# Routing eight late token tiles at the end of an attention, with a new weight layout, send order and pace of adds in the expert layer behind it

## The chip, the cores and the metric

The kernel runs on one core of a Trainium2 chip. The metric is the device time of one execution in microseconds (us). The core has engines that run their own instruction lists side by side: PE (TensorE, the matrix multiplier; PEld is its loading of weights), DVE (VectorE), ACT (ScalarE), POOL (GpSimd) and SP (SyncE, which here only issues transfers). An engine runs its list strictly in order: an instruction that waits for another engine or for a transfer (DMA) holds all that stand behind it. Transfers are carried by 16 DMA engines that all queues share.

## The reference, cut to what matters

The program is a stack of residual layers over 4096 tokens of 256 numbers, all in float32. The last one, which this change is about, is a mixture of 16 experts, of which each token uses four:

```python
x = x + _L1_attn_ref(_layernorm(x), ...)             # 16 heads, 8 sequences of 512 tokens
x = x + 0.5 * _L1_ffn_ref(_layernorm(x), ...)

def _L1_ffn_ref(x, gate_w, w1, w2, w3, ws1, ws2, ws3):
    scores = softmax(x @ gate_w.T)                   # 16 experts in 4 groups
    # keep the 2 groups with the largest best score, then the 4 best experts in them
    c = the scores of those four, 0 elsewhere        # [tokens, 16]
    a = silu(einsum('td,edi->tei', x, w1)) * einsum('td,edi->tei', x, w3)     # 128 hidden per expert
    y = einsum('tei,eid,te->td', a, w2, c)
    z = silu(x @ ws1) * (x @ ws3) @ ws2              # the shared expert, 256 hidden
    return y + z
```

Ahead of it stand an expert layer of another kind, an attention, the first expert layer again, this mixture of experts for a first time, and the attention named above (called the second attention here).

## The kernel before, in words

Tokens are held in SBUF as `x`, 32 *token tiles* of 128 tokens, one token on each of 128 partitions; four token tiles are a *group* (0 to 7, group 7 the last). A layer norm takes mean and variance of each row (`ln_mean`), then the inverse root of the variance, either with ACT's square root (`ln_root`, `ln_rest`) or with a shift and three Newton steps on DVE (`ln_guess`), and then normalizes the rows (`normal`).

*The second attention* (2236 to 3462 us in the profile) goes through 8 sequences. Between its matmuls it works off a list `todo` of small pieces, one or two per half chunk: adds of the previous mixture (`one.add`), means, roots, normalizations. It also routes the last layer ahead: the last layer's token tiles are cut into *part 0*, the first 20, and *part 1*, the last 12 (`LAST = 20, 12`). Once five sequences are through, `after.routing(0, ...)` runs piece by piece, and part 0's rows are sent. Logits of part 1's first eight tiles are also ready before the attention ends (`after.lg1`); those of the last four need the last sequence, whose output projection `project` is the attention's last work.

*Routing* (`Joint.routing`) is a generator that runs on DVE nearly alone; each `yield` is a place where the caller may put other work. It takes the softmax, picks two groups and four experts by repeated maximum (`topk`), counts each expert's tokens with two matmuls against constant triangles, works out for each token and each of its four experts a *slot*, and then `owner` (which expert a slot tile belongs to) and `coef` (the scores, halved). A slot tile is 128 slots of one expert. 143 slot tiles are held; part 0 fills tiles 0 to 63 for sure, tiles 64 to 95 take rows of both parts, tiles from 96 on have rows of part 1 alone.

*Sends* (`Joint.send`) write the normalized rows to their slots in DRAM: four indirect transfers from POOL per token tile, 48 for part 1. Each waits for the one before the last to have landed.

*The last layer* (`ffn1_after`, 3462 to 3889 us) has an order written out by hand, in which each engine's list is the order of the calls. In this order:

- SP's list: the weights of four experts, the first four loads of slot tiles (`xs`), the other experts' weights, the shared expert's weights.
- The tile loop, `for i in range(total)`: pass i is `step(i)`, which handles a pair of slot tiles at each of four stages: `hide(i-2)` multiplies with w1 and w3 and applies silu, `back(i-3)` transposes, `turn(i)` transposes the loaded rows, `give(i-4)` multiplies with w2 and writes the result `ys` to DRAM. So there are 72 pairs and 76 passes. Three results per pass are copied out of PSUM by `evict`, which alternates between DVE and ACT. Pair 32 is the first that is loaded after the sends of part 1 (its loads are issued in `turn(32)` and wait for all 48), and pass 51 is the one that writes pair 47, the last one with rows of part 0 (`known` is 48).
- Between the first passes: the root and normalization of group 7 after pass 2, its transposes (`columns`) and logits, and `routing(1, ...)`, four yields a pass; when it ends, the 48 sends are issued. The other groups are normalized again from then on, one every second pass.
- *Gathers and adds*: for each token tile four indirect transfers from POOL bring the four experts' rows into a buffer `yg` (four buffers), and four DVE instructions (line 1614) add them to `x` with their coefficients. `fetched(at)` does half of this: an even call adds the first half of the token tile three places earlier, an odd call adds the second half and issues the gather of a token tile. In the tile loop this starts at pass `known + 3`, in two of three passes, for part 0's 20 tiles at most.
- After the passes the shared expert, as 32 *units* that a `Pump` runs one by one (a unit's PE work goes ahead of the previous unit's DVE work): 8 groups of two `hidden` and two `outputs` units. Between units the remaining `fetched` calls are spread evenly. When a token tile has got both its adds and its shared part, it is written out (`done`).

## Time and profile before

| | us |
|---|---|
| four timed runs | 3902.15, 3902.30, 3903.89, 3892.21 |
| their median | 3902.23 |
| profiled execution | 3890.69 |
| its span, first to last instruction | 3889.0 |

The span by stages (columns: us, then busy time and instructions of PE, PEld, DVE, ACT and POOL, the granted clock of PE as a share of full speed, mean busy share of the 16 DMA engines, GB/s):

```profile
0.00:1750.00 1750.00, 1614.89 (x8912) 977.11 (x8912) 674.28 (x2291) 587.58 (x944) 594.18 (x498) 0.96 0.30 78
1750.00:2236.00 486.00, 407.32 (x1894) 322.39 (x1895) 228.76 (x549) 116.83 (x244) 216.04 (x221) 0.88 0.51 161
2236.00:3462.00 1226.00, 1215.34 (x5793) 655.50 (x5793) 749.04 (x1178) 644.58 (x1518) 238.26 (x215) 1.00 0.06 18
3462.00:3889.00 427.00, 371.54 (x1697) 290.53 (x1693) 210.26 (x482) 101.22 (x216) 198.69 (x208) 0.93 0.55 168
```

The rows are: the layers ahead, the mixture of experts for the first time, the second attention, and the last layer. PE is busy for 99% of the attention; in the last layer it stands for 55 of 427 us, its clock is a little below full there, and the DMA engines are busy for more than half of the time.

Two groups of instructions that the change touches (line, engine, operation, output and inputs, count, busy time, mean ns of one, idle time of the engine just before them and what ended it):

```profile
L1857 POOL DMA_INDIRECT slots_d<-wide,slot  x48 | 47.1, 980 | 131.3 <-DVE slot L1979 96.9 <-DMA slots_d<-wide,slot 27.8 <-issue 6.7
L2010 POOL DMA_INDIRECT yg<-ys_d,slot  x128 | 134.4, 1050 | 118.3 <-DMA ys_d<-ys 75.4 <-issue 32.6 <-DVE x L1614 3.8
```

The first are part 1's sends: POOL waited 96.9 us for slots and 27.8 us for earlier sends to land. The second are the gathers: POOL waited 75.4 us for the tile loop's results, and nearly no time for the adds.

### The profile page before, as it was taken

The page shows a single profiled execution, that of the slowest core. Times are in us where ns is not written, and L with a number is a line of the kernel's source. Part 1 is how long each engine was busy: PE and PEld are TensorE (multiplying, and loading weights), DVE is VectorE, ACT ScalarE, POOL GpSimd, SP SyncE. Part 2 cuts the span into 40 slices and gives each one's busy share as a digit, 9 for nine tenths or more (in the row PEclk, how much of TensorE's full clock was granted, in tenths as well). Part 3 has the DMA queues.
Part 4 walks back from the last instruction along what each step waited for, and adds up shares of the span by engine and source line. Part 5 has one row for each costly group of instructions (what it writes and reads, how often), then busy time and mean ns, then how long its engine had stood idle before and what let it go on. Part 6 is the DMA issues. An engine that isn't in the chain of part 4 may idle for free.

```text
span 3889.0 us, 51805 instructions
## 1 busy us (share of the span) xinstructions
PE 3609.1 (93%) x18293; PEld 2245.5 (58%) x18293; DVE 1862.3 (48%) x4500; ACT 1450.2 (37%) x2922; POOL 1247.2 (32%) x1142
## 2 busy tenths in 40 slices
PE   4999998999995999999769999999999999988988
PEld 1666664555542666666458845555555555557865
DVE  7221206666555221217324556666555567546355
ACT  3222223444444222222113355555554555532321
POOL 2333324333421333325832212220000102723177
PEclk7999999999997999998879999999999999999999
DMA  5444532001012233324446500000000000135564
GB/s 191 116 129 133 142 79 69 21 23 28 18 40 88 66 76 72 73 46 132 138 136 218 178 22 28 28 28 6 1 1 1 1 1 16 72 114 173 169 182 128
DMA packets 258173, 309.32 MB, mean 80 GB/s; under 512 B 34048, under 2 KB 227968, under 8 KB 257664
## 3 DMA queue, kind: packets, MB, share of 16 engines
q1 hardware_dynamic: 182144, 177.78, 14.6%
q0 software_dynamic: 49152, 101.24, 10.7%
q10 hardware_dynamic: 26624, 27.00, 2.1%
q8 instruction: 151, 2.47, 0.3%
q14 instruction: 102, 0.84, 0.1%
HBM read 159.51 MB, written 138.02 MB: 77 GB/s over the span
## 4 chain that ended last, share of the span: by engine, by line
PE 45%; issue 4%; DVE 3%; DMA 2%; POOL 2%; another core or an unknown queue 1%; ACT 1%; SPq 0%; POOLq 0%; DVEq 0%; ACTq 0%
PE sp L1110 6%; PE tp L1130 6%; PE pq L1088 6%; PE zp L1157 6%; PE hs L1786 3%; PE pv L1077 3%; PE hs L2073 3%; PE yp L1172 3%; PE yps L1808 2%; PE yps L2095 1%; PE hp L1708 1%; POOL yg L2010 1%; PE tpx L1772 1%; PE rp L1144 1%
## 5 line engine op out<-in xcount | busy, mean ns | idle before, releaser
L521 PE MATMUL hp<-exT,w 128*128 128x512 f32 x1024 | 451.8, 595 | 0.7 <-issue 0.7
L552 PE MATMUL op<-w,hid 128*128 128x256 f32 x2048 | 451.9, 379 | 0.0
L1119 ACT ACTIVATE ex<-sp,nmax 128x512 f32<-128x512 f32 x512 | 344.7, 685 | 238.9 <-DVE nmax L1116 230.5
L552 PEld LDWEIGHTS op<-w,hid 128*128 128x128 f32 x2048 | 386.8, 190 | 64.1 <-issue 14.3
L557 DVE TENSOR_TENSOR ob<-op,b 128x256 f32<-128x256 f32 x128 | 54.4, 425 | 642.8 <-PE op L552 535.0
L1116 DVE TENSOR_REDUCE nmax<-sp 128x2 f32<-128x1024 f32 x256 | 301.6, 1220 | 81.4 <-PE sp L1110 79.3
L531 POOL DMA_INDIRECT acc_d<-ob,idx x128 | 201.7, 1576 | 419.3 <-ACT ob L558 353.3
L812 DVE CUSTOM_DVE_ANT_0 junk<-sp,mask 128x128 bf16<-128x128 f32 (+3 forms) x512 | 251.1, 491 | 166.1 <-PE sp L803 142.0
L521 PEld LDWEIGHTS hp<-exT,w 128*128 128x128 f32 x1024 | 192.2, 190 | 220.4 <-issue 216.8
L1130 PEld LDWEIGHTS tp<-ident,ex 128*128 128x128 f32 x2048 | 233.9, 141 | 145.4 <-issue 87.3
L525 ACT ACTIVATE hid<-hp,b 128x512 f32<-128x512 f32 x256 | 175.9, 687 | 315.5 <-PE hp L521 315.5
L1130 PE MATMUL tp<-ident,ex 128*128 128x128 f32 x2048 | 272.9, 275 | 6.6 <-ACT ex L1119 4.1
L1601 POOL DMA_INDIRECT yg<-ys_d,slot x128 | 129.6, 1013 | 427.3 <-DVE x L1614 271.6
L1110 PE MATMUL sp<-qk,qk 64*128 64x512 f32 x1024 | 254.4, 615 | 0.0
L1088 PE MATMUL pq<-xnT,wide 128*128 128x512 f32 x512 | 247.5, 607 | 1.2 <-ACT xnT L250 0.8
L252 DVE COPY eT<-tp 128x512 f32<-128x512 f32 x256 | 177.0, 691 | 140.5 <-PE tp L1130 139.4
L1157 PE MATMUL zp<-eT,v 128*64 128x512 f32 x1024 | 234.0, 598 | 0.0
L250 ACT COPY eT<-tp 128x512 f32<-128x512 f32 x256 | 149.7, 585 | 220.5 <-PE tp L1130 189.6
L492 POOL DMA_INDIRECT ex<-xn_d,idx x128 | 131.4, 1026 | 294.7 <-DVE idx L483 260.6
L558 ACT ACTIVATE ob<-ob,gate 128x256 f32<-128x256 f32 x128 | 65.0, 508 | 414.0 <-DVE ob L557 364.0
L1059 POOL TENSOR_TENSOR x<-x,xn 128x1024 f32<-128x1024 f32 x8 | 18.9, 2362 | 544.7 <-DVE xn L1054 544.7
L855 ACT ACTIVATE ex<-st 128x1024 f32<-128x1024 f32 x160 | 155.1, 1022 | 95.0 <-PE st L848 95.0
(432 smaller groups left out, 6057.4 us busy)
## 6 DMA issues: line engine op xcount, KB each, us to landing
xs<-slots_d SPq DMA_DIRECT2D x149, 256.0 KB
ys_d<-ys SPq DMA_DIRECT2D x149, 256.0 KB
w<-in_W SPq DMA_DIRECT2D x32, 1024.0 KB
slots_d<-zero ACTq DMA_DIRECT2D x7, 2304.0 KB
w_sb<-in_w SPq DMA_DIRECT2D x24, 512.0 KB
xn_d<-xn SPq DMA_DIRECT2D x16, 512.0 KB
acc_d<-x SPq DMA_DIRECT2D x16, 512.0 KB
x<-acc_d SPq DMA_DIRECT2D x16, 512.0 KB
```

What stands on the lines that cost most here:

```text
L252: self.nc.vector.tensor_copy(out, in_)
L521: nc.tensor.matmul(hp, lhsT=w1[:, c, f * P : f * P + P], rhs=exT[e][:, c, h * CH : h * CH + CH], start=(c == 0), stop=(c == DC - 1),)
L525: nc.scalar.activation(hid[h][:, f, :], hp, AF.Gelu, bias=b1[:, e, f : f + 1])
L531: inst = nc.gpsimd.indirect_dma_start(out=acc_d[:, :], out_offset=bass.IndirectOffsetOnAxis(ap=idx[:, e, st : st + 1], axis=0), in_=ob, in ...
L552: nc.tensor.matmul(op, lhsT=hid[h][:, f, i * P : i * P + P], rhs=w2[:, f, :], start=(f == 0), stop=(f == FC - 1),)
L812: nc.vector.tensor_tensor_reduce(out=junk[:, :wd], in0=sps[h // 2][:, h % 2, at : at + wd], in1=mask[:, S - wd :], scale=1.0, scalar=NEG, ...
L1088: nc.tensor.matmul(pp, lhsT=(wq, wk)[a][:, k, c * P : c * P + P], rhs=xnT[b][:, k, :], start=(k == 0), stop=(k == DC - 1),)
L1110: nc.tensor.matmul(sp[:, j, :], lhsT=q[r, qt * P : qt * P + P], rhs=k[r, :], start=True, stop=True)
L1116: nc.vector.tensor_reduce(nmax, sp, AX.X, ALU.max, negate=True)
L1119: nc.scalar.activation(ex[:, j, :], sp[:, j, :], AF.Exp, bias=nmax[:, j : j + 1], accum_out=ch["sums"][:, qt, j : j + 1],)
L1130: nc.tensor.transpose(tp[:, k, :], ch["ex", qt][:, j, k * P : k * P + P], self.ident)
L1157: nc.tensor.matmul(zp[DK1 * j : DK1 * j + DK1, :], lhsT=v[b, h][:, k, at : at + DK1], rhs=ch["eT"][:, j, k, :], start=(k == 0), stop=(k == ...
```

## The change

1. The attention's roots use `ln_guess` in three pieces instead of ACT's square root in two; `ln_guess` becomes a generator `ln_guesses` for that.
2. The expert weights lie in DRAM by partition: w1 and w3 side by side in one array `w13`, w2 transposed. A load of four experts is two transfers instead of three. In the last layer SP issues w13 of twelve experts, the four loads of slot tiles, w13 of the last four, w2 in two halves, and then the shared expert's weights.
3. The choice of experts (`choose`, the first part of what was `routing`) runs for part 1's first eight tiles at the end of the attention, in turn with the last four `project` calls, eight yields each. `kept` gives its results a place that lasts (one of the `yg` buffers), and `Cut` makes buffers of full size of which a part is used. `routing(1, ...)` chooses for the last four tiles alone and then goes on for all twelve.
4. In the last layer pass 2 is issued after the root and normalization of group 7. While routing runs, `lean` sends all three evictions of a pass to ACT. Routing takes six yields a pass up to pass 6, then three, instead of four.
5. Sends of part 1: each waits for the third one before it instead of the second, and POOL clears a small buffer (`pause`) after every four. The last group's token tiles are sent first, and groups 5 and 6 are normalized within the list of sends.
6. Adds begin at pass `known + 5`. Between the shared expert's units at most one `fetched` call follows a unit, three in four units; what is left comes after the last unit.

The diff, cut to this:

```diff
@@ Kernel
     def ln_guess(self, pool, stats, t0, n):
+        for _ in self.ln_guesses(pool, stats, t0, n):
+            pass
+
+    def ln_guesses(self, pool, stats, t0, n):
...
             nc.vector.scalar_tensor_tensor(new, u, 1.5, y, ALU.add, ALU.mult)
             y = new
+            yield
@@ attn1
         def roots(ranges):
-            ys = []
-
-            def first():
-                for stats, t0, n in ranges:
-                    ys.append(self.ln_root(pool, stats, t0, n))
-
-            def second():
-                for (stats, t0, n), y in zip(ranges, ys):
-                    self.ln_rest(pool, stats, t0, n, y)
-            return [first, second]
+            guesses = [self.ln_guesses(pool, stats, t0, n) for stats, t0, n in ranges]
+            return [lambda g=g: next(g, None) for g in guesses for _ in range(3)]
...
+        after.kept()
+        ready = after.parts[1] - QT
+        early = after.choose(
+            after.lg1[:, :ready], Cut(front.pool, after.parts[0]), after.score1[:, :ready], after.hots1[:, :, :ready]
+        )
         for i in range(QT):
+            advance(early, 8)
             project(B - 1, i)
             self.ln_mean(self.late, after.stats, (B - 1) * QT + i)
+        for _ in early:
+            pass
@@ Grouped
-    def expert_weights(self, groups=range(4)):
+    def expert_weights(self, groups=range(4), back=True):
...
-            nc.sync.dma_start(
-                out=self.w13[:, es, :, 0:INTER], in_=w["w1"][es].rearrange("e (c p) i -> p e c i", p=P)
-            )
-            nc.sync.dma_start(
-                out=self.w13[:, es, :, INTER:], in_=w["w3"][es].rearrange("e (c p) i -> p e c i", p=P)
-            )
-            nc.sync.dma_start(out=self.w2[:, es], in_=w["w2"][es].rearrange("e p d -> p e d"))
+            nc.sync.dma_start(out=self.w13[:, es], in_=w["w13"][:, es])
+            if back:
+                nc.sync.dma_start(out=self.w2[:, es], in_=w["w2"][:, es])
+
+    def back_weights(self):
+        nc, w = self.k.nc, self.k.w
+        for h in range(2):
+            es = slice(h * 8, h * 8 + 8)
+            nc.sync.dma_start(out=self.w2[:, es], in_=w["w2"][:, es])
@@ Joint
     def send(self, h, t, row):
...
-            before = self.sent[-2:-1]
+            before = self.sent[-2:-1] if h == 0 else self.sent[-3:-2]
...
+        if h == 1:
+            nc.gpsimd.memset(self.pause, 0.0)
+
+    def kept(self):
+
+        t = self.k.late.tile([P, TOPK, D], F32, name="yg", bufs=2).rearrange("p r d -> p (r d)")
+        n = self.parts[1] * E1
+        self.score1 = t[:, :n].rearrange("p (t e) -> p t e", e=E1)
+        self.hots1 = t[:, n : n + TOPK * n].rearrange("p (r t e) -> p r t e", r=TOPK, e=E1)
...
+    def routing(self, h, lg, pool, row_psum, chosen=0):
...
+        if h == 0:
+            score = pool.tile([P, HT, E1], F32, name="score")
+            hots = pool.tile([P, TOPK, HT, E1], F32, name="hots")
+        else:
+            score, hots = self.score1, self.hots1
+        yield from self.choose(
+            lg[:, chosen:], Cut(pool, HT), score[:, chosen:], hots[:, :, chosen:]
+        )
@@ tile_steps: turn, back, give
-            k.evict(st[j]["xT"][:, :n], tp[:, :n], j)
+            k.evict(st[j]["xT"][:, :n], tp[:, :n], j | self.lean)
...
-            k.evict(st[j]["aT"][:, :n], tp[:, :n, :P], j)
+            k.evict(st[j]["aT"][:, :n], tp[:, :n, :P], j | self.lean)
...
-            k.evict(ys[:, :n], yp[:, :n], j + 1)
+            k.evict(ys[:, :n], yp[:, :n], (j + 1) | self.lean)
...
+class Cut:
+    def __init__(self, pool, room):
+        self.pool, self.room = pool, room
+
+    def tile(self, shape, dtype, name, bufs=1):
+        axis = 2 if len(shape) == 4 else 1
+        n, full = shape[axis], list(shape)
+        full[axis] = self.room
+        t = self.pool.tile(full, dtype, name=name, bufs=bufs)
+        return t[:, :, :n] if axis == 2 else t[:, :n]
@@ ffn1_after
+        f.lean = 0
         load, step, total, known = f.tile_steps()
-        f.expert_weights(range(1))
+        f.expert_weights(range(3), False)
         for j in range(4):
             load(j)
-        f.expert_weights(range(1, 4))
+        f.expert_weights(range(3, 4), False)
+        f.back_weights()
         f.shared_weights()
         g = TT // QT - 1
-        for i in range(3):
+        for i in range(2):
             step(i)
         k.ln_guess(f.route, f.stats, g * QT, QT)
         f.normal(g)
+        step(2)
         f.columns(g)
...
-        steps = f.routing(1, f.lg1, f.route, f.row_psum)
+        f.lean = 1
+        steps = f.routing(1, f.lg1, f.route, f.row_psum, f.parts[1] - QT)
+        advance(steps, 1)
...
-        begin, at, ends = known + 3, 0, 2 * (len(order) + 3)
+        begin, at, ends = known + 5, 0, 2 * (len(order) + 3)
         rest = list(range(g)[::-1])
-        for i in range(total):
-            if i >= 3:
-                step(i)
+        for i in range(3, total):
+            step(i)
             if not sending:
-                sending = not advance(steps, 4)
-                if i < 2:
-                    f.normal(rest.pop(0))
+                sending = not advance(steps, 6 if i < 7 else 3)
                 if sending:
-                    for t in range(f.parts[1]):
+                    f.lean = 0
+                    f.pause = f.route.tile([P, CH], F32, name="pause")
+                    tokens = list(range(f.parts[1]))
+                    for t in tokens[-QT:] + tokens[:-QT]:
+                        if t % QT == 0 and t < tokens[-QT]:
+                            f.normal((a + t) // QT)
+                            rest.remove((a + t) // QT)
                         f.send(1, t, f.xn[:, a + t, :])
-                    pause = f.route.tile([P, TOPK, f.parts[1], E1], F32, name="hots")
-                    f.pause = pause.rearrange("p r t e -> p (r t e)")[:, :CH]
...
-        units, done_units, from_ = len(pump.units), 0, at
+        units, from_ = 0, at
         while pump.units or pump.pending:
             pump.run(1)
-            done_units += 1
-            while at < ends and (at - from_) * units < (ends - from_) * done_units:
+            units += 1
+            if at < ends and 4 * (at - from_) < 3 * units:
                 fetched(at)
                 at += 1
@@ weights on the host
-        "w1": i["L1_ffn_w1"],
-        "w3": i["L1_ffn_w3"],
-        "w2": i["L1_ffn_w2"],
+        "w13": np.concatenate([i["L1_ffn_w1"], i["L1_ffn_w3"]], axis=2).reshape(E1, DC, P, 2 * INTER).transpose(2, 0, 1, 3),
+        "w2": i["L1_ffn_w2"].transpose(1, 0, 2),
```

More of the change, by code (lines that the diff above doesn't have):

```diff
@@ L1870, in send, with choose @@
             self.of_part[h].append(inst)
-    def routing(self, h, lg, pool, row_psum):
+        if h == 1:
[5 more added lines that the diff above has]
+        self.hots1 = t[:, n : n + TOPK * n].rearrange("p (r t e) -> p r t e", r=TOPK, e=E1)
+    def choose(self, lg, pool, score, hots):
         k, nc = self.k, self.k.nc
-        HT = self.parts[h]
+        HT = lg.shape[1]
         GS = E1 // N_GROUPS
-        score = pool.tile([P, HT, E1], F32, name="score")
         m = pool.tile([P, HT], F32, name="m", bufs=2)
@@ L1900, in routing @@
         yield
-        hots = pool.tile([P, TOPK, HT, E1], F32, name="hots")
         yield from k.topk(pool, masked, E1, TOPK, hots)
+    def routing(self, h, lg, pool, row_psum, chosen=0):
+        k, nc = self.k, self.k.nc
+        HT = self.parts[h]
+        if h == 0:
[6 more added lines that the diff above has]
+        )
         chosen = pool.tile([P, E1, HT], F32, name="chosen")
@@ L1912, in routing @@
         flat = "p e t -> p (e t)"
-        carry = pool.tile([P, E1, HT], F32, name="masked")
+        carry = pool.tile([P, HT, E1], F32, name="masked").rearrange("p t e -> p (t e)").rearrange("p (e t) -> p e t", e=E1)
         nc.vector.memset(carry, 1.0)
@@ L1919, in routing @@
         nc.tensor.matmul(pb, lhsT=k.ones, rhs=chosen.rearrange(flat), start=True, stop=True)
-        inc = pool.tile([P, E1, HT], F32, name=f"left{E1}")
+        inc = pool.tile([P, HT, E1], F32, name=f"left{E1}").rearrange("p t e -> p (t e)").rearrange("p (e t) -> p e t", e=E1)
         nc.vector.tensor_tensor_scan(inc.rearrange(flat), carry.rearrange(flat), pb, 0.0, ALU.mult, ALU.add)
```

## The prediction

> **What bounds the kernel now.** I read the page's slices first: PE is busy 9 tenths or more nearly everywhere from 2300 us to 3450 us, and gaps return in the last stage, which the change edits. So I split that stage by windows (columns: us, then busy time of PE, PEld, DVE, ACT and POOL, the granted clock, DMA share, GB/s).
>
> ```profile
> 3476.00:3533.00 57.00, 35.07 (x152) 28.63 (x150) 36.17 (x120) 12.34 (x22) 1.05 (x1) 0.79 0.38 111
> 3533.00:3614.00 81.00, 80.35 (x428) 69.94 (x426) 39.13 (x89) 25.92 (x59) 46.00 (x47) 0.96 0.68 220
> 3614.00:3689.00 75.00, 71.52 (x379) 62.72 (x378) 25.81 (x52) 23.26 (x53) 0.20 (x1) 0.95 0.52 161
> 3689.00:3775.00 86.00, 75.03 (x369) 61.89 (x368) 47.80 (x102) 22.01 (x53) 64.29 (x68) 0.94 0.66 194
> 3775.00:3889.00 114.00, 95.57 (x314) 55.65 (x312) 57.56 (x112) 17.70 (x31) 87.15 (x92) 0.95 0.43 128
> ```
>
> In the first window PE does 35 us of work in 57 us, at a clock of 0.79. Its timeline names the waits (start, duration, instruction, idle before it and releaser):
>
> ```profile
> 3484.66 3.75 PE L2073 MATMUL hs<-w_sb,xT 128*128 x8 [6.65 <-DMA w_sb<-in_w]
> ...
> 3492.73 2.21 PE L1679 MATMUL tp<-ident,wide 128*128 128x128 f32 x8 [3.58 <-DVE wide L1484]
> ...
> 3512.58 0.69 PE L2087 MATMUL tpa<-ident,as 128*128 128x128 f32 x2 [7.66 <-DVE aT L252]
> ```
>
> PE waits for weights, then for a normalization that stands behind them on DVE, then for DVE, which is busy routing. From 3533 to 3614 PE is full: one pass of the tile loop is 3.25 us (turn, hide, back and give of two slot tiles). Then come the sends and the gathers, on POOL's timeline:
>
> ```profile
> 3531.92 1.05 POOL L1857 DMA_INDIRECT slots_d<-wide,slot  x1 [96.86 <-DVE slot L1979]
> ...
> 3612.44 0.97 POOL L1857 DMA_INDIRECT slots_d<-wide,slot  x1 [0.30 <-issue]
> 3688.80 1.07 POOL L2010 DMA_INDIRECT yg<-ys_d,slot  x1 [75.39 <-DMA ys_d<-ys]
> ...
> 3881.79 1.01 POOL L2010 DMA_INDIRECT yg<-ys_d,slot  x1 [0.30 <-issue]
> ```
>
> The sends wait for DVE's slots, pass 32 waits for the last send (PE stands 2.64 us at 3617.77 and is at half clock for a pass: pass 33 begins at 3624.96, 7.2 us later instead of 3.25). The gathers start when the tiles with rows of part 0 are written (pass 51, 3683.66), and 32 tokens' worth then run on POOL with hardly a gap, 193 us, to the end. So the end is the start of the gathers plus a fixed chain, and that start hangs on how soon slots come and how fast sends and passes go. The chain of waits agrees: gathers and "issue" alternate in it from 3776 on.
>
> **The change part by part.** Times are those of the profiled span (3889.0 us).
>
> *Square roots in the attention.* The 13 Sqrt calls with their table changes (L192 and L1119, 8 loads each of 1283 ns, 20.5 us of ACT) become ln_guess on DVE: 12 small operations of 0.195 us each, start to start, instead of 6, so 1.2 us more DVE a call. It pays only where PE waits. PE's idle from 2246 to 3460 us is 10.7 us (6.6 at L1130, 2.0 at L1144, 0.8 at L1088, 1.3 at L1996), and ACT's 52% and DVE's 62% of these stages hide both sides. Bounds -10.7 and, if every call's 1.2 us came late, +15.6; I take -1, since PE is above 98% there. The third piece per call moves the rows of the next batch one or two half chunks later in the list, still two ahead of the transposes that use them.
>
> *Weights by partition.* In the first FFN the 12 loads become 8; L1786, which uses them, starts 100 us later: 0. In the last one, 5.2 MB (w13 and four slot tiles) stand ahead of the first hs instead of 6.8 MB. In the windows of the load they moved at 308 GB/s, with the queues full:
>
> ```profile
> 3470.00:3476.00 6.00, 6.00 (x29) 5.30 (x28) 2.02 (x6) 0.00 (x0) 0.00 (x0) 1.00 1.14 308
> ```
>
> From about 3459 us that is 17 us; at the fastest window of the trace with such loads (352 GB/s at 1750-1760 us) 15 us. Either way they are there by 3476-3478.
> The Trainium skill speaks against any gain from longer runs: "DMA: Bandwidth & Descriptors", section Specifications, has 512 B as the smallest transfer at line rate, which the old pieces already are. By it the rate stays, by longer runs it might rise, and the sum is the same, as DVE is later.
>
> *Early choice at the attention's end.* 44 DVE operations for 8 tiles now stand between the last adds. Rows for 48 elements are 0.21 us and for 192 elements 0.36 us; between them 128 elements cost about 0.29, with 0.035 to the next: 30 x 0.325 + 14 x 0.225 = 12.9 us, of 14 us in which DVE did 4. I place them: 5.6 us after zn (3463.6), the first add at 3469.2, 4.6 us, second add, 2.6 us, and the last add is done at 3480.8 instead of 3478.0. Cost 2.8 us; the project matmuls reuse a bank only at 3473, so PE is not held.
>
> *Start of the stage.* xT then lands at 3481.5 and the first hs starts there, not at 3484.66. What is worth more: ln_guess no longer stands behind that pass's product on DVE (10.32 us idle before L2081 at 3488.86). It runs 3481.5-3483.8, the four rows until 3485.2, turn and logits as before 6.1 us (3492.73 to 3498.82), so the logits are there at 3491.5 instead of 3498.8: -7.3 us.
> PE still stands about 4 us before that first hs. The trace shows what such a gap did: hs took 3.75 us after 6.65 us idle and 1.89 us in a full pass. The Trainium skill ("TensorE: Matmul & The Clock Gate", HAM oscillation) states the rule behind it, that idle gaps over some 3.4 us halve the clock; by it the half clock stays, as I assumed, and without it the logits come 2 to 4 us sooner.
>
> *Logits to slots.* Before 32.6 us (3498.8 to 3531.45). The choice shrinks from 12 tiles (30 x 0.39 + 14 x 0.24 = 15.1 us) to 4 (30 x 0.255 + 14 x 0.20 = 10.5): -4.6. Two normalizations of 1.38 us move behind it: -2.7; they are needed 16 sends later, about 23 us, which hides them. Evictions go to ACT (lean): -2.9 on DVE; ACT then does 1.9 us of each 3.25 us. Two more passes' products: +0.8. DVE alone gives 23.2 us; passes in between make it wait. Bounds 23 and 30, I take 26.5: slots at 3518.0, 13.4 us earlier.
>
> *Sends in threes, with a pause.* Before, twos: (3612.44 - 3531.92) / 47 = 1.71 us, 6.85 us a token. With three flying and a 0.54 us pause the part sends at 1888 to 1990 us (L1493) took 5.56 us a token, on quieter queues. Bounds 5.56 and 6.85 + 0.71 = 7.56; I take 5.9, near the first, as POOL's waits here are mostly under 1 us. Last send at 3518.4 + 11 x 5.9 + 3.9 = 3587.2; before, pass 32 began 5.3 us after the last send: 3592.5. PE itself: 29 passes of 3.25 us from the second hs (3492.2) is 3586.4, plus 8 us of routing passes held by DVE and 3 us behind the coefficients: 3597. So PE decides, the stand and its half clock at pass 32 go, and pass 33 begins at 3600.3 instead of 3624.96: -24.7 us.
>
> *Adds: begin + 5 and three in four units.* The gathers still wait only for the written tiles, not for begin. Pass 51 begins at 3600.3 + 18 x 3.25 = 3658.8, the first gather 5.4 us later as before. A token costs POOL 5.8 us (18 tokens, 3776.80 to 3883.3, less 2.3 us of waits). Adds two passes later meet landed rows: add t stands at 22 + 4.9 t us after pass 51 begins, its rows land at 12 + 5.8 t, equal at t = 11, so DVE and PE are no longer held as at 3698-3732. Passes end 65 + 11 = 76 us after pass 51. The 32 units of the shared expert follow: a group is 12.0 us with its transposes (3850.96 to 3862.99) and 10.5 without, 7 x 12.0 + 10.5 = 94.5 us. At three half adds in four units a token has 7.9 us where POOL needs 5.8, so POOL falls idle late in the stage, and gathers 28 to 31 are issued after the last unit: 3 x 5.8 + 3.9, and 7.2 us from the last gather to the end. Together 76 + 2 + 94.5 + 28.5 = 201 us; before 3889.0 - 3683.7 = 205.3. If POOL were never held: 5.4 + 31 x 5.8 + 3.9 + 7.2 = 196; if units were as slow as before (105.7 us) 212. I take 202, -3.
>
> Sum: -24.7 - 3 - 1 = -29, less a little for passes that DVE holds: -28, a span of 3861 us. The profiled execution took 3890.69 us, the span and 1.7 us around it; the median of the four runs is 11.5 us above it (three lie at 3902 to 3904). Against the median: 3902.2 - 28 = 3874 us.
>
> **The rivals.** *Sends stay the bound.* For: POOL waited for landed sends before half of them, with DMA share 0.68, and the pause adds 8.5 us. At 7.56 us a token pass 32 begins at 3518.4 + 83.2 + 3.9 + 5.3 = 3610.8, with the half clock pass 33 at 3618.0: -7, with the tail -3: 3892 us. Against: with three flying a send may take three intervals to land.
> *The pace starves the gathers (slower).* Place: the shared units, PE's order, from which adds and so POOL's buffers hang. 24 half adds are tied to units, four tokens wait for the last. Each 0.1 us more a unit costs 3.2 us at the end; from a mean of 3.8 us, against 2.95 worked out and 3.3 before, it eats the gain of 25. At 4.1 us: 3902 + 37 - 25 = 3914 us. For it: DVE waits for rows at the stage's start. Against: rows land earlier than the adds come.
> *Routing is not sooner.* If DVE and the passes wait on each other (each pass now carries two of three evictions less, but more routing), logits to slots stays at 33 us and sends are no faster: about 3895-3902, within measurement.
>
> **How the numbers follow.** Forecast 0.70 (own range 3856 to 3888), sends bound 0.12, starving 0.10, no sooner 0.08. About 0.2% (8 us) is what a measurement can tell from no change: faster 0.82 (the forecast and most of the sends rival), same 0.08, slower 0.10. The low end takes the bounds together (slots 3.5 us sooner, tail -9, attention -5, half clock gone) and runs at the lower group of the four: 3852; the high end reaches the sends rival and part of the last: 3895.
>
> **What would show it.** First hs near 3481 with at most some 4 us idle; slots near 3518; sends near 5.9 us a token; no wait at pass 32 (xs); pass 51 near 3659; no PE gaps where 3698-3732 had them; POOL idle behind x late in the shared units and four gathers after PE's last matmul. Wrong it is if PE waits for xs at pass 32, if the first hs waits for w_sb, or if PE's end comes later than 175 us after pass 51.

## The result and the profile after

The changed kernel took 3909.66 us (median of 52 runs, 3879.71 to 3933.03). The kernel before, run on the same chip, took 3896.89 us (78 runs, 3867.30 to 3917.66). The ratio is 1.0037 with a 95% interval of 1.0025 to 1.0049: slower by 0.37%, where 28 us less had been forecast. The profiled execution took 3941.34 us (span 3939.6), 32 us above its median, so its lines show the loss larger than it usually is; other profiles of the same kernel follow below. Of the 50.6 us between the two profiles' spans, 18.5 lie ahead of the attention's last projection, and the largest part in them is that the first mixture's first `hs` comes 177 us after the last matmul of the layer ahead of it, where it was 150; more on this below.

First the same windows of the last layer as before, cut at the same events (end of the attention, first send, last send, first gather, end of the passes; columns: us, busy time of PE, PEld, DVE, ACT and POOL, granted clock, DMA share, GB/s):

```profile
3495.00:3533.00 38.00, 31.96 (x171) 26.90 (x170) 28.55 (x112) 17.88 (x34) 0.00 (x0) 0.96 0.42 135
3533.00:3600.00 67.00, 35.18 (x143) 26.47 (x142) 18.83 (x48) 8.06 (x18) 53.32 (x59) 0.77 0.44 147
3600.00:3725.00 125.00, 122.09 (x639) 106.19 (x638) 47.66 (x99) 39.60 (x90) 0.64 (x2) 0.94 0.49 153
3725.00:3813.00 88.00, 74.53 (x374) 62.52 (x373) 47.05 (x101) 23.09 (x53) 65.97 (x71) 0.92 0.65 193
3813.00:3939.00 126.00, 94.23 (x312) 55.63 (x310) 58.97 (x114) 17.76 (x31) 83.03 (x90) 0.87 0.39 114
```

The first row is the gain: 38 us from the attention's end to the slots, where there were 57, and PE works in it. The second row is the loss. The sends take 67 us instead of 81, but PE, which was full before (80.35 of 81 us), is busy for 35 us at a clock of 0.77, and has done 143 matmuls instead of 428. So after the last send there are still 125 us of passes until the first gather, where there were 75.

PE's timeline in that second row, and where the passes meet the loads (start, duration, instruction, idle time before it and its releaser):

```profile
3499.48 1.99 PE L2099 MATMUL hs<-w_sb,xT 128*128 x8 [1.58 <-DMA ws_sb<-in_ws]
...
3551.20 1.89 PE L2099 MATMUL hs<-w_sb,xT 128*128 x8
...
3556.39 1.89 PE L2099 MATMUL hs<-w_sb,xT 128*128 x8
3565.15 0.69 PE L2113 MATMUL tpa<-ident,as 128*128 128x128 f32 x2 [6.88 <-issue]
...
3568.99 3.78 PE L2099 MATMUL hs<-w_sb,xT 128*128 x8
3580.11 0.69 PE L2113 MATMUL tpa<-ident,as 128*128 128x128 f32 x2 [7.34 <-DVE aT L257]
...
3599.17 0.69 PE L2113 MATMUL tpa<-ident,as 128*128 128x128 f32 x2 [12.62 <-issue]
...
3654.99 1.11 PE L2084 MATMUL tpx<-ident,xs 128*128 128x128 f32 x4 [2.35 <-DMA xs<-slots_d]
```

PE stands before each transpose of `as` (`tpa`). It needs two things: DVE's product, and, as `tpa` has one buffer, the copy `aT` of the transpose before it. The product needs ACT's silu (`sgs`), and that the matmuls `hs`. In the order of a pass, `hide(i-2)` and then `back(i-3)`, the transpose at 3565.15 works on the `hs` of the pass before, which ended at 3553.09 (3551.20 and 1.89) and not on the one that ended at 3558.28. ACT's and DVE's timelines show when they saw it:

```profile
3563.25 0.38 ACT L2105 ACTIVATE sgs<-hs 128x256 f32<-128x256 f32 x1 [7.20 <-remote]
3564.73 0.37 ACT L255 COPY aT<-tpa 128x256 f32<-128x256 f32 x1 [1.09 <-remote]
3571.12 0.59 ACT L255 COPY ys<-yps 128x512 f32<-128x512 f32 x1 [6.02 <-remote]
```

```profile
3559.66 0.69 DVE L257 COPY ys<-yps 128x512 f32<-128x512 f32 x1 [5.96 <-PE hs L2099]
3563.67 0.42 DVE L2107 TENSOR_TENSOR as<-sgs,hs 128x256 f32<-128x256 f32 x1 [3.31 <-ACT sgs L2105]
```

ACT, idle for the last 7.20 us, starts this silu 10.16 us after its `hs` ended; "remote" says that the profile found no releaser. DVE's product then follows ACT by 0.04 us, and PE's transpose follows the copy `aT` by 0.05 us. Each pass has one `hs` and one silu, and every profile has 152 of both in the two mixtures, so they can be paired by count: the silus of the next three passes come 19.2, 22.4 and 16.2 us after their `hs`, and once the sends are over they come after 0.04 us again, as they do before 3549 us. In between, the hand-overs from PE to another engine are late, and none between the others.

POOL's timeline (sends, then gathers):

```profile
3533.50 1.05 POOL L1864 DMA_INDIRECT slots_d<-wide,slot  x1 [73.47 <-DVE past L2011]
3534.86 1.43 POOL L1864 DMA_INDIRECT slots_d<-wide,slot  x1 [0.30 <-issue]
...
3599.12 0.98 POOL L1864 DMA_INDIRECT slots_d<-wide,slot  x1 [0.30 <-issue]
...
3725.70 1.08 POOL L2036 DMA_INDIRECT yg<-ys_d,slot  x1 [125.07 <-DMA ys_d<-ys]
...
3905.52 1.02 POOL L2036 DMA_INDIRECT yg<-ys_d,slot  x1 [4.52 <-DVE x L1619]
...
3933.43 1.01 POOL L2036 DMA_INDIRECT yg<-ys_d,slot  x1 [0.30 <-issue]
```

Sends follow each other without a wait (65.6 us for 47, 1.40 us each, where it was 1.71). The gathers end 207.7 us after they begin, where it was 193, because POOL now waits for adds late in the stage (4.52 us and more).

Where the passes went can be read from the semaphore events of the trace. Each matmul that signals was matched, in order, with the next event of PE's semaphore (a part of the events is missing in the trace, of ACT's here more than half, so it is an approximation). This is how long after the matmul's end the event came:

```
                                        signals   over 0.5 us late   mean us   longest
before, attention                PE        1138                  0      0.02
before, part 1's sends           PE          64                  6      0.11       1.0
after, part 1's sends            PE          22                 17     10.57      22.4
after, part 1's sends            ACT          8                  0      0.01
after, part 1's sends            DVE         21                  0      0.01
before, first mixture 1880-1995  PE          40                 30     11.14      36.4
```

The pairs of `hs` and silu, of which none is missing, say the same for part 1's sends: 0.08 us on average before, 0.7 at most, and 8.85 us after, 22.4 at most.

The last row is the clue. The kernel before has the same lateness, in the first mixture of experts, whose sends were in threes with a clearing after every four all along. There its profile, which was at hand, shows PE busy for half of the time:

```profile
1880.00:1990.00 110.00, 53.95 (x204) 40.03 (x202) 13.52 (x25) 9.99 (x22) 86.69 (x98) 0.71 0.42 141
```

That row was the source of the price of 5.56 us a token in the prediction.

### The profile page after: what moved, and what is told of

It reads as the page before. It is cut to its first block, busy times and chain, and to the rows that moved or that the text cites. A ratio compares the mean times of both kernels' runs of the same rounds, so it can differ in the third digit from the quotient of the medians.

```text
span 3939.6 us, 51902 instructions
## 1 busy us (share of the span) xinstructions
PE 3621.8 (92%) x18293; PEld 2251.1 (57%) x18293; DVE 1876.5 (48%) x4612; ACT 1434.1 (36%) x2903; POOL 1249.1 (32%) x1154
## 3 DMA queue, kind: packets, MB, share of 16 engines
q0 software_dynamic: 49152, 101.24, 10.7%
## 4 chain that ended last, share of the span: by engine, by line
PE 45%; issue 5%; DVE 3%; another core or an unknown queue 2%; POOL 1%; DMA 1%; ACT 1%; POOLq 0%; SPq 0%; DVEq 0%; ACTq 0%
PE sp L1115 6%; PE tp L1135 6%; PE zp L1162 6%; PE pq L1093 6%; PE hs L1793 3%; PE pv L1082 3%; PE hp L1715 3%; PE yp L1177 3%; PE hs L2099 2%; PE yps L1815 2%; PE yps L2121 1%; PE yp L1741 1%; POOL yg L2036 1%; PE tpx L1779 1%
## 5 line engine op out<-in xcount | busy, mean ns | idle before, releaser
L1606 POOL DMA_INDIRECT yg<-ys_d,slot x128 | 130.0, 1016 | 414.9 <-DVE x L1619 259.3
L2036 POOL DMA_INDIRECT yg<-ys_d,slot x128 | 131.7, 1029 | 185.3 <-DMA ys_d<-ys 125.1
```

## The experiments

Ratios are to the kernel before, run on the same chip in the same session, with 95% intervals. The chips differ: the kernel before took 3928 us beside e1 to e4, 3897 beside e9 to e12 (both chip 13), 3901 beside e13 to e16 (chip 14) and 3819 beside e5 to e8 (chip 5).

### e1, e2, e3, e4: the sends and the pace

e1 is the changed kernel unedited. e2 puts the sends back to twos:

```diff
-            before = self.sent[-2:-1] if h == 0 else self.sent[-3:-2]
+            before = self.sent[-2:-1]
```

e3 leaves the threes and clears after each send:

```diff
             self.of_part[h].append(inst)
-        if h == 1:
-            nc.gpsimd.memset(self.pause, 0.0)
+            if h == 1:
+                nc.gpsimd.memset(self.pause, 0.0)
```

e4 has the old pace:

```diff
-        begin, at, ends = known + 5, 0, 2 * (len(order) + 3)
+        begin, at, ends = known + 3, 0, 2 * (len(order) + 3)
...
-            if at < ends and 4 * (at - from_) < 3 * units:
+            while at < ends and (at - from_) * units < (ends - from_) * done_units:
```

> The changed kernel once more, for a second profile. Theory A (signals): while POOL issues part 1's sends back to back, three in flight, PE's completion signals reach ACT and DVE late, by chance more or less; then PE again stands for 15 us or more between the first and the last send, and the ratio to the kernel before is 1.002 to 1.006. Rival B (pace): PE runs through the sends with under 5 us idle, and the time is lost behind pass 51, with 215 us or more from there to the end (205 before). Rival C (chance): the first profile was an odd execution; then neither shows and the ratio is near 0.995.

> The changed kernel with part 1's sends in twos again, as before; the pause stays. A: POOL waits for landings again, 6.9 to 7.5 us a token instead of 5.5; PE's idle time between the first and the last send falls under 8 us (it was about 31 us of the 65 us from 3535 on), pass 32 starts some 10 us before that of the kernel before, and the time falls by 15 to 30 us against the changed kernel: ratio 0.995 to 0.999. B: no gain from it, sends are only slower: 0 to 10 us more than the changed kernel, ratio 1.004 to 1.007. C: as B.

> The changed kernel with the 0.54 us clearing on POOL after every single send of part 1 instead of after every fourth; still three in flight. A token then costs POOL about 7.6 us, 1.9 us a send. If it is the rate at which POOL issues sends that delays PE's signals, PE's idle time between the first and the last send falls under 8 us as with twos, and the time is that of twos within 5 us. If it is the three in flight (more transfers landing at once), PE still stands 15 us or more there, and with the slower sends the ratio is 1.004 or more. B and C: PE has no idle time to lose there, ratio 1.004 to 1.007.

> The changed kernel with the old pace of adds: begin at pass known + 3, and the half adds spread evenly over the shared expert's units. A: the stalls at the sends stay; from pass 51 to the end 205 to 212 us; the time moves by less than 10 us either way. B: the tail falls to 205 us and the time with it by 15 us or more: ratio 0.998 or less. C: no difference to the changed kernel beyond its scatter.

Measured: e1 1.0055 (1.0032 to 1.0078), e2 0.9970 (0.9952 to 0.9987), e3 0.9970 (0.9953 to 0.9987), e4 1.0027 (1.0009 to 1.0045). The window from the first to the last send of part 1, of e1, e2, e3 in this order (columns as above):

```profile
3548.80:3615.20 66.40, 32.62 (x140) 25.16 (x141) 18.25 (x44) 7.78 (x18) 52.42 (x59) 0.82 0.44 146
```

```profile
3535.30:3619.10 83.80, 74.42 (x408) 65.30 (x408) 40.98 (x92) 25.23 (x58) 52.39 (x59) 0.97 0.62 204
```

```profile
3548.20:3628.70 80.50, 75.89 (x408) 66.39 (x408) 45.18 (x92) 25.31 (x58) 71.70 (x94) 0.98 0.65 213
```

With 14 to 17 us more for the sends, PE does 408 matmuls in them instead of 140. Theory A holds, and chance (C) falls: e1 shows the stall again. One half of B's sign shows too, a tail of more than 215 us behind pass 51 in e1 (216.6 from the first gather alone). Against e1 the two slower orders win 0.85% by the ratios (medians 3952.58 us for e1, 3913.63 for e2, 3920.76 for e3), 39 and 32 us, where 15 to 30 were expected of e2. e3's sends came every 1.71 us, and not 1.9 as expected. PE's idle time is 33.7 us in e1, 9.4 in e2 and 4.6 in e3 (e2 missed its mark of 8). Most of what is left in e2 is another wait. PE comes to pass 32 at 3611.82, before the last send has gone out, and stands for that pass's loads until 5.3 us after the last send's start. This is pass 32 in e2, and in e14 (below), whose sends are faster:

```profile
3624.42 1.12 PE L2084 MATMUL tpx<-ident,xs 128*128 128x128 f32 x4 [12.60 <-DMA xs<-slots_d]
```

```profile
3599.80 1.11 PE L2084 MATMUL tpx<-ident,xs 128*128 128x128 f32 x4 [2.39 <-DMA xs<-slots_d]
```

So with twos the sends bound pass 32 (e3 stands there for 6.84 us), and the gain is what PE saves in spite of that. The pace (B) costs something too: e4 is 0.28% under e1 (medians 12.8 us apart, where A expected under 10), but the intervals overlap, and its profile has a tail as long as the others (213.7 us), so this run alone doesn't settle it.

### e5, e6, e7, e8: a second profile before, both steps undone, and the early choice

e6 is e2 with the pace of e4. e7 is e6 with the first mixture's sends in twos too:

```diff
-            before = self.sent[-3:-2]
+            before = self.sent[-2:-1]
```

e8 is e2 without the early choice (the block behind `after.kept()` taken out, and):

```diff
-        steps = f.routing(1, f.lg1, f.route, f.row_psum, f.parts[1] - QT)
+        steps = f.routing(1, f.lg1, f.route, f.row_psum)
```

> The kernel before once more, for a second profile. If PE's signals are late by chance wherever POOL issues transfers back to back, the first mixture (sends in threes in both kernels) shows it here too: about 177 to 184 us from the last matmul of the layer ahead to the first hs, as in all profiles of the changed kernel, and not the 150 us of the first profile of before. If the new weight layout causes it there, this profile shows 150 us again. In the last layer 410 to 415 us from the attention's last projection to the end, and 200 to 206 us from the first gather to the end.

> The changed kernel with sends in twos and with the old pace of adds (begin at known + 3, spread evenly). If the new pace costs 10 to 15 us at the tail (216 us from the first gather to the end in three profiles, 200 in that of before), the first gather stays 198 us after the attention and the end comes 200 to 206 us later: ratio 0.992 to 0.995, 8 to 15 us under sends in twos alone (0.997). If the tail is set by late signals during the gathers and not by the pace, the tail stays at 212 us or more and the ratio at 0.996 to 0.999.

> As e6, and the first mixture's 128 sends in twos instead of threes as well. If back-to-back sends delay PE's signals there too, PE's idle time in that mixture's tile loop (63 to 71 us in the profiles so far) falls by 20 us or more; the sends themselves get slower by some 0.3 us each, 16 us for the first part. Net 0 to 30 us less than e6: ratio 0.985 to 0.994. If the sends' rate bounds that stage, it is 5 to 20 us slower than e6.

> Sends in twos, and without the early choice: routing chooses for all twelve token tiles after the attention, as before (the other orders of the change stay). If the early choice is what brings the slots 15 to 17 us sooner (38 to 41 us after the attention's last projection, 55 before), they come at 50 to 56 us here, pass 32 moves with them, since it waits for the last send, and the time is 10 to 16 us above sends in twos alone (0.997): ratio 1.000 to 1.002. If the order of the stage alone brings it, the ratio stays at 0.996 to 0.998.

Measured: e6 0.9936 (0.9917 to 0.9955), e7 1.0008 (0.9995 to 1.0020), e8 0.9967 (0.9954 to 0.9980). On this chip the first mixture's loop takes 275 us in e5, e6 and e8, where it takes 331 to 347 us in all profiles with its sends in threes on the others; PE idles in it for 15 us instead of 52 to 71. Paired as above, the silus follow their `hs` within 0.04 us through all of these sends on chip 5 (e8: 1.44 us a send), where in the profile before, at 1.45 us a send, they come 11.6 us late on average. So how much PE stands there differs from chip to chip, or from session to session (chip 5 was used in one alone), and the spacing is not all of it. e12 below, with the old weights on chip 13, has the loop at 333 us like the others, so the new weights don't make the loop.

The stretch ahead of the loop, which e5 was to settle, stays open. From the last matmul of the layer ahead to the first `hs` it is 152 us in e5, as in the first profile, but 150 to 152 with the new weights on chip 5 too. On the other chips, with threes, it is 166 to 184 us with the new weights, 150 and 158 with the old ones (the first profile, e12), and 160 and 153 with the new ones and spaced sends (e13, e15). So the slower sends shorten it there, and the new weights may lengthen it; two profiles with the old ones don't show it. e5's last layer was shorter than expected: 407 us behind the last projection (410 to 415) and 195 from the first gather (200 to 206).

e6 wins as expected: the tail from the first gather is 197.5 us, and 205.1 in e8, which differs from it in the pace and the early choice. e8 refutes what its text supposed first: without the early choice the first send comes 39.1 us after the attention's last projection, with it 38.5 (55.5 in the kernel before). So the rest of the change brings the slots forward, not the early choice. e7's forecast, 0.985 to 0.994, failed on this chip: where no signal is late, slower sends only cost, and the loop takes 297 us, 22 more.

### e9, e10, e11, e12: the same chip for all, the roots and the weights

e9 is the changed kernel again, e10 is e6 again. e11 is e6 with the old `roots` (ACT's square root, two pieces), e12 is e6 with the three old weight arrays and, in the last layer, the old order:

```diff
-        f.expert_weights(range(3), False)
+        f.expert_weights(range(1))
         for j in range(4):
             load(j)
-        f.expert_weights(range(3, 4), False)
-        f.back_weights()
+        f.expert_weights(range(1, 4))
```

> The changed kernel beside three others on one chip. The chips differ: the first mixture's tile loop took 338 to 347 us on those of e1 to e4 (kernel before 3928 us) and 275 us on that of e5, e6 and e8 (kernel before 3819 us), with PE idle in it for 63 to 71 us on the ones and 15 on the other. If that is how much PE's signals are late under back-to-back sends, a chip of the first kind gives 25 us or more of idle PE between part 1's first and last send and a ratio of 1.003 to 1.006; one of the second kind gives under 15 us of it, only the tail's 8 us stay lost, and the ratio is 0.994 to 0.999. If sends in threes cost the same everywhere, it is 1.003 or more on either kind.

> Sends in twos and the old pace, as e6, beside the changed kernel on the same chip. 0.991 to 0.996 on either kind of chip, if the rest of the change is worth 12 us in the last layer and 5 in the attention; on a chip of the first kind 0.8% or more below e9, on one of the second kind 0.2 to 0.5% below it.

> As e10, with the square roots on ACT in the attention again. If the roots are what shortened the attention (from its first score matmul to its last projection 1236 us in both profiles of the kernel before, 1230 to 1232 in those with the change), it takes 1235 to 1238 us here and the time is 4 to 7 us above e10. If the early choice or something else did it, the attention stays at 1230 to 1232 us.

> As e10, with the old weight arrays, the old twelve transfers and their old order. If the layout and order bring the first hs forward (4 to 4.5 us after the attention's last projection, 8.2 in the kernel before), it comes at 7 to 9 us here; group 7's transposes stand behind it on PE, so slots and pass 32 come 3 to 5 us later and the time rises by 3 to 5 us. My prediction took the layout alone as nothing; if that holds for the order too, hs stays under 5.5 us and the time within 2 us of e10.

Measured: e9 1.0042 (1.0015 to 1.0070), e10 0.9955 (0.9931 to 0.9980), e11 0.9954 (0.9928 to 0.9979), e12 0.9962 (0.9939 to 0.9985). PE stood 24.6 us between e9's sends, just under the 25 expected. The two sizes that were wrong, sends and pace, are worth 0.87% together on one chip by the ratios (medians 3912.57 us for e9, 3878.88 for e10). Roots and weights can't be told from nothing by the time. By the profiles the attention takes 1236.7 us with ACT's roots and 1230.5 without, as expected, and its idle PE time is 10.7 and 7.1 us; the 6 us don't show in the medians (3881.36 and 3878.88), whose intervals are some 10 us wide on either side. With the old weights the first `hs` comes 8.5 us after the last projection instead of 4.5, and slots and pass 32 come 6.7 and 5.6 us later, where 3 to 5 were expected; the median is 5.2 us higher, within the noise.

### e13, e14, e15, e16: spacing alone

e13 is e6 with a clearing after each send of the first mixture (still threes); e14 is e4 with a clearing after every second send of part 1:

```diff
-        if h == 1:
-            nc.gpsimd.memset(self.pause, 0.0)
+            if h == 1 and r % 2 == 1:
+                nc.gpsimd.memset(self.pause, 0.0)
```

e15 is e7 again, e16 the changed kernel again.

> As e6 and e10 (sends in twos in the last layer, old pace), and in the first mixture a clearing on POOL after each send instead of after every fourth (still threes): 1.7 us a send instead of 1.4. If spacing alone keeps PE's signals on time, PE's idle time in the first mixture's tile loop falls from 52 to 71 us to under 40 on chip 13; the loop takes 295 to 310 us instead of 333, the first part's sends 14 us longer: ratio 0.985 to 0.992. On chip 5, where that loop takes 275 us, it gets longer by about 20 us as in e7, and the ratio is 0.998 to 1.002. If signals are late whatever the spacing, the ratio is above 1.000 on either.

> The changed kernel with the old pace, and a clearing on POOL after every second send of part 1 (still threes): about 1.55 us a send, between 1.40, where PE stands for 25 to 34 us on chip 13, and 1.71, where it stands for 1 to 10. If lateness grows with the rate by degrees, PE stands for 8 to 20 us, ratio 0.995 to 1.000; if there is a point between 1.40 and 1.71 from which signals are late, it is under 8 or over 25.

> e7 once more, beside e13 on one chip: sends in twos in both mixtures. On chip 5 it lengthened the first mixture's loop by 22 us (297 for 275). On chip 13 twos should free PE as spacing does: ratio within 0.3% of e13's, 0.985 to 0.993. On chip 5 again 1.000 to 1.002.

> The changed kernel as a measure for the three beside it. On chip 13 the ratio is 1.003 to 1.007 as three times before; on chip 5, where the first mixture's loop hardly stands, PE's idle time between part 1's sends stays under 15 us, and only the 8 us of the tail are lost: 0.993 to 0.999.

Measured: e13 0.9838 (0.9803 to 0.9873), e14 0.9961 (0.9940 to 0.9983), e15 0.9809 (0.9775 to 0.9844), e16 1.0047 (1.0024 to 1.0070). Both e13 and e15 are a little better than expected. The first mixture's loop in e16, e13 and e15, in this order:

```profile
1904.50:2237.30 332.80, 277.75 (x1401) 236.39 (x1402) 125.17 (x273) 88.73 (x200) 127.21 (x136) 0.90 0.56 179
```

```profile
1903.40:2204.50 301.10, 261.65 (x1400) 230.11 (x1401) 124.63 (x273) 88.28 (x199) 163.34 (x198) 0.92 0.62 199
```

```profile
1888.30:2185.80 297.50, 262.84 (x1400) 230.71 (x1401) 124.79 (x273) 88.34 (x199) 132.23 (x142) 0.93 0.62 201
```

The same work takes 32 to 35 us less with the sends spaced, by clearings (POOL busier) or by waits. And part 1's sends in e14 and e16:

```profile
3516.30:3587.80 71.50, 67.64 (x365) 58.51 (x366) 37.35 (x83) 21.76 (x49) 59.27 (x70) 1.00 0.69 227
```

```profile
3517.70:3583.50 65.80, 38.98 (x154) 29.95 (x154) 20.14 (x49) 8.22 (x19) 52.46 (x58) 0.77 0.46 155
```

Six more us for the sends more than double the matmuls that PE does in them. Nine profiles together, with the time from a send's start to its landing divided by the spacing as the number in flight, and the time from the end of an `hs` to its silu, paired by count, for PE's signals:

```
                       us a send   in flight   silu after its hs: mean, longest (us)   PE idle in the sends (us)
changed: after              1.40        1.74               8.85    22.4                   31.7
changed: e1                 1.41        1.79               9.75    25.0                   33.7
changed: e9                 1.41        1.79               6.71    19.0                   24.6
changed: e16                1.40        1.79               8.04    24.7                   26.8
e4, old pace                1.40        1.77               9.48    25.3                   28.6
e14, clearing per two       1.52        1.86               0.61     2.8                    3.8
before, twos                1.71        1.73               0.08     0.7                    1.1
e3, clearing per one        1.71        1.64               0.04     0.0                    4.6
e2, twos                    1.78        1.66               0.04     0.1                    9.4
```

It isn't the number in flight: e14 has more than any other and its signals are nearly on time, and the kernel before has as many as the changed one. Nor is it the traffic as a whole: the DMA engines moved 227 GB/s in e14's sends and 155 in e16's. On these chips the spacing decides, and most of the lateness is gone at 1.52 us: e14's idle time lies under the 8 to 20 us that its text expected if lateness grew by degrees. In e14 PE, and not the sends, decides when pass 32 begins, 122.0 us after the last projection, close to the 120.5 forecast, and earlier than with twos. The clearing is not to blame, since most of it (e3, e13) goes with the best signals.

## Why the prediction was wrong, point by point

- *Start of the stage, logits, slots: right.* Times from the attention's last projection matmul, forecast and measured: first `hs` 5.0 and 4.5 us, logits 15.0 and 12.3, slots 41.5 and 38.3. The early choice had been priced at 4.6 us saved behind the attention and 2.8 paid in it; e8 says 0.6 net.
- *The rate of the sends: right in itself.* 5.9 us a token forecast, 5.6 measured.
- *"So PE decides, the stand and its half clock at pass 32 go": this is the step that failed.* It let PE run 29 passes of 3.25 us beside the sends. Pass 32 was to come 120.5 us after the last projection, and came at 155 to 161 us in four profiles of the changed kernel (141 before); with twos it comes at 128 to 129 us in e2, e6 and e10. The price of the sends came from a stretch with the same spacing, "on quieter queues", without a look at what PE did there. Two of the prediction's own signs of being wrong show: the wait for `xs` at pass 32, and PE's end some 190 us after pass 51. The small half of the sentence was wrong too: pass 32 issues its own loads, so PE waits 2.35 us for them even when all sends have landed 50 us earlier, and runs at half clock behind that (`yps` 2.07 us instead of 1.03). The rule that the prediction cites from the Trainium skill ("TensorE: Matmul & The Clock Gate", HAM oscillation), that gaps over some 3.4 us halve the clock, holds for the stands of 6.9 us and more here (`hs` takes 3.78 us behind one, and 1.89 in a full pass); behind this shorter gap the clock was halved too.
- *The tail: mis-sized.* From the first gather to the end 196.6 us were forecast and 202.5 to 217.9 measured with the new pace in seven profiles (mean 212.0). Of nine profiles with the old pace in the changed stage, seven have 195.7 to 198.5 us and two more (209.5 and 213.7). The units and the four last tokens were sized right (94.5 and 28.5 us forecast; 93.9 from the first hidden matmul and 29.5 measured). What failed is "DVE and PE are no longer held": passes end 86.5 us after the first gather (73.8 to 92.9 in the other six), 86.2 before, where 71 were forecast. PE's signals are late during the gathers as well, in both kernels: from the first gather on, silus come 1.99 us after their `hs` on average in the profile before and 2.42 in e16. The profiles go with this as the cause, though no run changes it alone: where silus are on time (0.04 us in the four profiles of chip 5, 0.36 in e9) passes end 74 to 82 us after the first gather, and 74 in the two of these with the new pace; where they are late by 1.4 to 3.0 us on average they end 79 to 100 us after it. With signals on time the new pace still has the longer tail, 202.6 us in e9 and 205.1 in e8, where the old one has 197.5 in e6: it pays 21 us behind the last unit (29.5 for 8.4) and gets back some 8 in the units.
- *Weights: the layout was taken at nothing.* The window of the load shows 308 GB/s before, 306 in e12 (3472 to 3478 us), and this after:

```profile
3489.00:3495.00 6.00, 6.00 (x30) 5.28 (x29) 5.42 (x20) 0.00 (x0) 0.00 (x0) 1.00 1.02 420
```

  So the new arrays did move faster, where the prediction, by the Trainium skill ("DMA: Bandwidth & Descriptors", Specifications), let the rate stay; with the order they are worth 6.7 us to the slots (e12), part of what was forecast for the start of the stage.
- *Roots:* 1 us forecast, 6 us in the profiles, not resolved by the time.
- *The rivals.* None named the cause. "The pace starves the gathers" had the sign and part of the place (adds hold POOL), but its price, slower units, did not come; "sends stay the bound" had the stage, but with POOL as the engine that is late, when it was PE; it is what comes about once the sends are in twos (e2).

With both failing steps undone, the rest of the change is worth 0.45% to 0.64% (e10, e6), 18 to 24 us where 28 were forecast.

## What to carry to other kernels

When a price is borrowed from another stretch of the trace, read the whole stretch: what the other engines did in it is part of the price. A faster queue of indirect transfers is only a gain if the engines that run beside it keep their pace; look for hand-overs from PE that start microseconds after the matmul's end, with a releaser that the profile can't name. Pair each with its own matmul by count: in a loop that works on several passes at once, the last matmul before it is often that of another pass. Some 0.3 us more between POOL's sends was worth more on chips 13 and 14 than the rest of the change (0.45% in e10): e15, with twos in both mixtures, is 1.9% under the kernel before on chip 14 (medians 3826.08 and 3900.89 us), and e13 1.6%; on chip 5 e7, the same kernel as e15, gains nothing, and e6 is the best there.

## What the runs showed of the hardware

PE's completion signals, 0.02 us behind the matmul's end in the attention, came up to 47 us late (first mixture in e3) on chips 13 and 14 while POOL issued indirect transfers of 128 rows every 1.4 us, and were on time at 1.7 us (e2, e3, e13); ACT's and DVE's signals came within 0.01 us on average in the four profiles matched for them (before, after, e2, e9). On chip 5 they were on time at 1.44 us too (silus 0.04 us behind `hs` in e8); the same stretch cost PE 15 us instead of 52 to 71, and this explains much of why the kernel before took 3819 us there and 3897 to 3928 elsewhere (its loop in the first mixture alone is 66 us shorter, 275.1 for 340.8).

Why it is PE alone was not found. The Trainium skill, page "Perfetto Trace Analysis", section "Tensor Engine Instruction (MATMUL, LD_WEIGHTS)", says that the end of a matmul in a profile is estimated and that its signal goes out only once PSUM has acknowledged the writes. So the records here can't tell a late signal from a matmul that really ended late. Every timed run has a span and a clock and so was recorded as well; whether it is the same without recording, no run tells.
